# Grouped attention on one Trainium2 core: maxima and sums spread by VectorE's transposes, and a normalisation moved one step

## The chip, the cores and the metric

The kernel runs on one core of a Trainium2 chip. The metric is device time in microseconds (us) of one launch. The engines are named as the profile names them: PE is the tensor engine (PEld its weight loads), DVE the vector engine, ACT the scalar engine, POOL the GpSimd engine, SP the engine that issues most of the DMAs. PSUM is the memory that PE writes; it has 8 banks here of 512 float32 each on 128 partitions.

## The reference

Four cross-attention layers follow each other on x (4 batches, 512 queries, 256 channels), all with the same context (4 batches, 1024 rows, 512 channels). Layers 0, 2 and 3 have 16 heads of 64; four columns of their logits get a bias made from two masks. They are called masked here. Layer 1 has 16 query heads of 16 that share 4 heads of keys and values; it is called grouped.

```python
# layers 0, 2, 3
logits = einsum('bhqd,bhkd->bhqk', q, k) * scale + col_bias
probs = softmax(logits, axis=-1)
out = einsum('bhqk,bhkd->bhqd', probs, v)      # then @ Wo + bo + residual
# layer 1, after an RMS norm of x
scores = einsum('btgrd,bsgd->bgrts', qg, k) * scale
attn = softmax(scores, axis=-1)
out = einsum('bgrts,bsgd->btgrd', attn, v)     # then @ wo + residual
```

All of it is float32.

## The kernel before, in words

**Units and steps.** The work is cut into units: a pair of heads of a masked layer (8 units per layer and batch), or, in the grouped layer, one of the four query heads of each group (r) for one half of the four groups (h = 0 or 1), also 8 per batch. A written table (MASKED_TURNS, GROUPED_TURNS) sets them into 96 steps. Each step has one masked unit (g in the code); 32 of the steps have a grouped unit too (lam). The eight grouped units of a batch lie in eight steps on end, h = 0 and h = 1 in turn, so there are four such stretches. The loop at line 968 issues a step's instructions engine by engine in program order; no scheduler moves them afterwards. So the order of the calls is the order of each engine's queue.

**A step with a grouped unit.** First come the scores of the masked unit (line 643): for each of eight tiles of 128 keys PE makes the logits (L653), ACT copies them to SBUF (L663), and DVE keeps a running maximum in PSUM (L667). Then follow, woven together, the masked unit of the step before against its values (attend, L685) and the grouped unit's logits (logits_pair, L617) with their exponentials (L640). Meanwhile DVE reduces the masked maximum (L713, L721, L738), sums the exponentials of the previous unit over the partitions (reciprocal_sums, L713 to L821), scales that unit's output (L830, scale_out), spreads the maximum (L745) and subtracts it tile by tile (L750); ACT takes the exponentials (L756) and POOL adds them up (L795). Beside that PE works through a list (fill): query projections (L549), output projections (L845, added to the state by L867), the grouped unit against its values (L685, 32 columns), keys (L473), values (L515). Between these stand the four pairs of logits of the next grouped unit, which are only for its maximum (maxima_pair, L617 again, with L607 on ACT and L609 on DVE).

**The grouped maximum.** The softmax's maximum over all keys must be taken from the queries before the exponentials. max_columns (line 724) reduces the running maximum over partitions with a turning reduction (L713) and small maxima (L721, four of L730) into eight columns. In the next step, inside scores after the sixth tile (`within`, line 669), lower_queries (line 623) spreads them: sixteen small matmuls per unit against the identity (line 630) fill one PSUM bank, and DVE multiplies it by a column that is -1 in row 16 of each block of 32 and adds it to the queries (L635).

**The grouped sum.** The values have a column of ones, so row 16 of each 32 rows of the output o holds the sum of the exponentials. After an h = 1 unit both halves of o are there, and normalise_grouped runs at the end of that step (line 1160): one matmul with sel spreads row 16 over its 32 rows (sums_grouped, L705), then DVE turns it (L571), takes the reciprocal of one column in 32 (L572), turns it back (L573) and multiplies (L800). The result, ot, is projected in the next step.

**PSUM.** All eight banks belong to one tile; the class Place (line 96) hands out one or two of them, those given back longest ago first, with a preference for a bank whose neighbour is in use. back() stamps the return with a count. An instruction that writes a bank waits for the last reader of it.

Of the kernel before, what the change touches and what calls it, by code (L numbers as in the profile page):

```python
# [12 lines left out]
ALU = mybir.AluOpType  # L13
# [3 lines left out]
P = 128  # L17
B, S, C = 4, 512, 256
# [58 lines left out]
def kernel(ctx: ExitStack, tc: tile.TileContext, a: dict, out: bass.AP):  # L77
# [8 lines left out]
    def t_(shape, tag, name, bufs=1, dtype=FP):  # L86
        return sb.tile(shape, dtype, tag=tag, name=name, bufs=bufs)
# [8 lines left out]
    class Place:  # L96
# [11 lines left out]
                del free[n]  # L108
            self.ap = ps_all[:, at : at + width, :].rearrange("p n q -> p (n q)")

        def back(self):
            returns[0] += 1
            for n in self.banks:
                given_back[n] = returns[0]


    st_all = t_([P, 2, NT + 1, 2 * S], "st", "st")
# [1 line left out]
    def st_slot(n):  # L119
# [8 lines left out]
    nc.vector.memset(ones, 1.0)  # L128
    eps = t_([P, 1], "eps", "eps")
    nc.vector.memset(eps, EPS)  # L130

    sel = t_([P, 4, 32], "sel", "sel")
    nc.vector.tensor_copy(
        sel, ident.rearrange("p (g d) -> p g d", d=32)[:, :, 16:17].to_broadcast([P, 4, 32])
    )


    row16 = t_([P, 2], "row16", "row16")
    nc.vector.reduce_sum(
# [425 lines left out]
    def reciprocal_rows(out_, in_, room):  # L565


        turned = room[:, 0:S]
        short = t_([P, S // 32, 1], "short", f"short{len(turns)}")
        turns.append(0)  # L570
        nc.vector.transpose(turned, in_)  # L571
        nc.vector.reciprocal(short, turned.rearrange("p (c r) -> p c r", r=32)[:, :, 0:1])  # L572
        nc.vector.transpose(  # L573
            out_.rearrange("p (c r) -> p c r", r=32), short.to_broadcast([P, S // 32, 32])
        )
# [44 lines left out]
                )  # L620
        return ws

    def lower_queries(g):

        w = Place(1)
        m = w.ap
        for n in range(NI):
            for c in range(4):
                column = NI * (c % 2) + n
                nc.tensor.matmul(  # L630
                    m[32 * c : 32 * (c + 1), n * P : (n + 1) * P],
                    lhsT=g.mcol[:, column : column + 1].to_broadcast([P, 32]), rhs=ident,
                    start=True, stop=True,
                )
        nc.vector.scalar_tensor_tensor(g.qt, m, row16[:, 1:2], g.qt, ALU.mult, ALU.add)  # L635
        w.back()

    def exponentials_pair(g, i):
        for odd, w in enumerate(logits_pair(g, i)):
            nc.scalar.activation(g.st[2 * i + odd], w.ap, AF.Exp)  # L640
            w.back()

    def scores(g, within):
        g.st = [st_slot((NT + 1) * g.ring + t) for t in range(NT)]
        g.mx = st_slot((NT + 1) * g.ring + NT)
        g.mx_place = Place()
        for t in range(NT):

            w = Place() if t else g.mx_place
            m = w.ap  # L650
            keys = slice(t * P, (t + 1) * P)
            for j in range(2):
                nc.tensor.matmul(  # L653
                    m[:, j * S : (j + 1) * S], lhsT=g.kt[g.rows[j], keys], rhs=g.qt[g.rows[j], :],
                    start=True, stop=t > 0,
                )
            if t == 0:
                for j in range(2):
                    nc.tensor.matmul(  # L659
                        m[:, j * S : (j + 1) * S], lhsT=aug_k[g.l][g.rows[j], keys],  # L660
                        rhs=aug_q[g.rows[j], :], start=False, stop=True,
                    )
            nc.scalar.copy(g.st[t], m)  # L663
            if t:
                w.back()
                top = g.mx_place.ap
                nc.vector.tensor_tensor(top, top, g.st[t], ALU.max)  # L667
            if t == 5:
                within()

    def place_out(g, width=1):
        g.place = Place(width)
# [26 lines left out]
        nc.vector.tensor_tensor(half, half, g.po[64:128, :], ALU.add)  # L699
        g.place.back()  # L700

    def sums_grouped(g):
        g.place = Place(1)
        g.psum = g.place.ap
        nc.tensor.matmul(  # L705
            g.psum, lhsT=sel.rearrange("p g d -> p (g d)"), rhs=gq[g.b, "o"], start=True, stop=True
        )

# [12 lines left out]
        nc.vector.tensor_tensor(half, quarter[0:64, :], quarter[64:128, :], ALU.max)  # L721
        return half

    def max_columns(g):

        half = max_halves(g, g.mx)
        g.mcol = t_([P, 2 * NI], "mcol", f"mcol_{g.name}", bufs=3)
        of = half.rearrange("x (c h) -> x h c", h=4)
        for h in range(4):
            nc.vector.tensor_tensor(  # L730
                g.mcol[32 * h : 32 * (h + 1), :], of[0:32, h, :], of[32:64, h, :], ALU.max
            )

    def max_quarters(g):
        half = max_halves(g, g.mx_place.ap)
# [6 lines left out]
    def max_everywhere(g):  # L742
        g.mb_place = Place()
        g.mb = g.mb_place.ap
        nc.vector.transpose(  # L745
            g.mb.rearrange("p (b r) -> p b r", r=32), g.every.to_broadcast([P, 2 * S // 32, 32])
        )
# [55 lines left out]
    def reciprocal_sums(g):  # L803

        w = Place(1)
        quarter, half = w.ap[:, 0:32], w.ap[0:64, 32:64]
# [11 lines left out]
        w.back()  # L818
        nc.vector.reciprocal(short, short)
        g.ot = t_([P, S], "ot", f"ot_{g.name}", bufs=3)  # L820
        nc.vector.transpose(  # L821
            g.ot.rearrange("p (c r) -> p c r", r=32), short.to_broadcast([P, S // 32, 32])
        )

    def normalise(g):
        reciprocal_sums(g)
        scale_out(g)

    def scale_out(g):
# [133 lines left out]
    attended = None  # L963
    count = 0
    ready = []
    left = {b: 32 - 4 for b in range(B)}

    for n in range(len(steps) + 2):
# [46 lines left out]
        def pair(i):  # L1015
            if i == 0:
                behind_exponentials()
            maxima_pair(coming, i)
            if i == NT // 2 - 1:
                max_columns(coming)  # L1020

        if coming:
            share(coming)
# [12 lines left out]

        if g:
            g.now = NT if masked_at(g.n + 1) else 4
            scores(g, lambda: lower_queries(lam) if lam else None)

        ending = n >= len(steps) - 2
        if g1 and (g or lam):
# [1 line left out]
        if g:  # L1044
            max_quarters(g)
            if not lam:
                g.mx_place.back()
                max_everywhere(g)
        if lam:
# [103 lines left out]
        while pairs:  # L1153
            pair(pairs.pop(0)[1])
        behind_exponentials()
        if coming and not follows:
            lower_queries(coming)
# [36 lines left out]
```

## Time and profile before

| | us |
|---|---|
| median of 3 runs | 3774.69 (3774.36 to 3774.75) |
| the profiled execution | 3773.92 |
| its span in the profile | 3772.2 |
| DVE wait for L705 (L571), 4 times | 41.4 |
| 32 x L635 on DVE | 23.9 |
| 16 x L800 on DVE | 11.1 |
| 96 x L745 on DVE | 120.7 |

The profile page lists busy time by engine, a chain of work that ended last, and groups of instructions by line. A group row reads: line, engine, operation, what it writes and reads, shapes, count, then busy time and mean nanoseconds of one, then idle time of the engine just ahead of it and what ended it. A timeline row reads: start and length in us from the span's start, engine, line, operation, count, and in brackets the idle time before it and its releaser. A float32 matmul appears as two records. The granted TensorE clock is 0.998 of full speed over the whole execution.

### The profile page before, as it was taken

The page shows a single profiled execution, that of the slowest core. Times are in us where ns is not written, and L with a number is a line of the kernel's source. Part 1 is how long each engine was busy: PE and PEld are TensorE (multiplying, and loading weights), DVE is VectorE, ACT ScalarE, POOL GpSimd, SP SyncE. Part 2 cuts the span into 40 slices and gives each one's busy share as a digit, 9 for nine tenths or more (in the row PEclk, how much of TensorE's full clock was granted, in tenths as well). Part 3 has the DMA queues.
Part 4 walks back from the last instruction along what each step waited for, and adds up shares of the span by engine and source line. Part 5 has one row for each costly group of instructions (what it writes and reads, how often), then busy time and mean ns, then how long its engine had stood idle before and what let it go on. Part 6 is the DMA issues. An engine that isn't in the chain of part 4 may idle for free.

```text
span 3772.2 us, 50461 instructions
## 1 busy us (share of the span) xinstructions
PE 3723.8 (99%) x19662; PEld 1860.2 (49%) x19662; DVE 3000.4 (80%) x3928; ACT 2104.1 (56%) x2433; POOL 1625.0 (43%) x749
## 2 busy tenths in 40 slices
PE   8999999999999999999999999999999999999998
PEld 4555544445444444444555555554544445555554
DVE  6887787877887778787888888888787778888888
ACT  4555555555555555555555555555555555555554
POOL 3555333343333433333555555555333335555554
PEclk9999999999999999999999999999999999999999
DMA  2111110001000010000000110000100000000100
GB/s 68 42 31 28 39 28 21 18 20 25 22 19 21 12 33 19 22 21 18 26 26 26 43 42 24 25 26 22 26 19 23 20 24 26 26 26 26 31 25 8
DMA packets 187875, 98.71 MB, mean 26 GB/s; under 512 B 43241, under 2 KB 183529, under 8 KB 187637
## 3 DMA queue, kind: packets, MB, share of 16 engines
q1 hardware_dynamic: 182510, 82.90, 8.0%
q0 software_dynamic: 2560, 8.39, 0.8%
q10 hardware_dynamic: 2566, 4.20, 0.5%
q8 instruction: 155, 2.54, 0.3%
q14 instruction: 84, 0.68, 0.1%
HBM read 89.16 MB, written 2.10 MB: 24 GB/s over the span
## 4 chain that ended last, share of the span: by engine, by line
PE 86%; DVE 9%; issue 2%; ACT 2%; DMA 0%; DVEq 0%; POOL 0%; ACTq 0%; POOLq 0%
PE ps L515 19%; PE ps L685 18%; PE ps L473 17%; PE ps L653 12%; PE ps L617 7%; DVE ps L667 6%; PE ps L845 5%; PE ps L549 5%; ACT st L663 2%; DVE st L750 1%; PE ps L491 1%; DVE qt L635 1%; PE ps L659 1%; PE ps L705 0%; PE ps L379 0%
## 5 line engine op out<-in xcount | busy, mean ns | idle before, releaser
L795 POOL TENSOR_TENSOR st<-st 128x1024 f32<-128x1024 f32 x668 | 1580.5, 2366 | 2088.3 <-ACT st L756 2044.0
L667 DVE TENSOR_TENSOR ps<-ps,st 128x1024 f32<-128x1024 f32 x672 | 828.2, 1232 | 462.8 <-ACT st L663 405.5
L756 ACT ACTIVATE st<-st 128x1024 f32<-128x1024 f32 x768 | 783.0, 1054 | 650.0 <-DVE st L750 636.2
L750 DVE TENSOR_TENSOR st<-st,ps 128x1024 f32<-128x1024 f32 x768 | 885.9, 1214 | 3.3
L685 PE MATMUL ps<-st,v 128*64 128x512 f32 x4064 | 810.9, 598 | 0.0
L663 ACT COPY st<-ps 128x1024 f32<-128x1024 f32 x768 | 716.1, 1044 | 107.3 <-PE ps L659 82.3
L515 PEld LDWEIGHTS ps<-wv,ctx 128*128 128x128 f32 x6400 | 729.4, 192 | 80.9 <-issue 64.6
L515 PE MATMUL ps<-wv,ctx 128*128 128x128 f32 x6400 | 744.8, 276 | 0.6 <-ACT st L663 0.6
L653 PE MATMUL ps<-qt,kt 64*128 64x512 f32 x3072 | 710.5, 598 | 0.0
L473 PE MATMUL ps<-ctx,wk 128*128 128x512 f32 x1536 | 693.3, 599 | 2.2 <-ACT ctx L385 2.2
L685 PEld LDWEIGHTS ps<-st,v 128*64 128x64 f32 x4064 | 231.2, 130 | 551.5 <-issue 491.6
L473 PEld LDWEIGHTS ps<-ctx,wk 128*128 128x128 f32 x1536 | 285.7, 190 | 395.7 <-issue 375.0
L653 PEld LDWEIGHTS ps<-qt,kt 64*128 64x128 f32 x3072 | 282.7, 186 | 323.8 <-ACT st L663 142.2
L527 ACT COPY v<-ps 128x512 f32<-128x512 f32 x200 | 117.2, 586 | 538.2 <-PE ps L515 538.1
L609 DVE TENSOR_TENSOR st<-st,ps 128x1024 f32<-128x1024 f32 x224 | 273.5, 1221 | 128.1 <-ACT st L607 70.7
L640 ACT ACTIVATE st<-ps 128x1024 f32<-128x1024 f32 x256 | 248.1, 1021 | 180.2 <-PE ps L617 139.8
L617 PE MATMUL ps<-qt,kt 32*128 32x512 f32 x2048 | 302.6, 639 | 16.1 <-DVE qt L635 12.8
L845 PE MATMUL ps<-ot,wo 128*128 128x512 f32 x448 | 214.6, 607 | 0.7 <-DVE ot L830 0.7
L549 PE MATMUL ps<-x,wq 128*128 128x512 f32 x384 | 185.5, 606 | 1.1 <-ACT x L357 1.1
L617 PEld LDWEIGHTS ps<-qt,kt 32*128 32x128 f32 x2048 | 91.0, 183 | 191.0 <-ACT st L640 52.2
L478 ACT COPY kt<-ps 128x512 f32<-128x512 f32 x192 | 110.3, 574 | 102.8 <-PE ps L473 102.6
L845 PEld LDWEIGHTS ps<-ot,wo 128*128 128x128 f32 x448 | 79.8, 189 | 129.2 <-issue 120.0
(143 smaller groups left out, 1629.9 us busy)
## 6 DMA issues: line engine op xcount, KB each, us to landing
wk<-in_L_xattn_Wk_dram SPq DMA_DIRECT2D x96, 256.0 KB, 2.9
wv<-in_L_xattn_Wv_dram SPq DMA_DIRECT2D x96, 256.0 KB, 2.7
wq<-in_L_xattn_Wq_dram SPq DMA_DIRECT2D x96, 128.0 KB, 2.8
wo<-in_L_xattn_Wo_dram SPq DMA_DIRECT2D x96, 128.0 KB, 2.9
qt<-qt ACTq DMA_DIRECT2D x32, 128.0 KB, 2.2
xraw<-in_x_dram SPq DMA_DIRECT2D x3, 512.0 KB
out_dram<-out SPq DMA_DIRECT2D x3, 512.0 KB
wq<-in_L_xattn_wq_dram SPq DMA_DIRECT2D x32, 32.0 KB, 3.4
```

Of the source, the lines that this page charges most:

```text
L473: nc.tensor.matmul(m, lhsT=g.wk[:, k, :], rhs=ctx_t[g.b][:, k, n * 512 : (n + 1) * 512], start=(k == 0), stop=(k == KT - 1),)
L515: nc.tensor.matmul(m[:, t * P : (t + 1) * P], lhsT=ctx_t[g.b][:, k, (4 * n + t) * P : (4 * n + t + 1) * P], rhs=g.wv[:, k, :], start=(k == ...
L549: nc.tensor.matmul(m, lhsT=g.wq[:, k, :], rhs=x[:, k, :], start=(k == 0), stop=(k == KC - 1))
L617: nc.tensor.matmul(ws[odd].ap[:, j * S : (j + 1) * S], lhsT=g.kt[rows, i * P : (i + 1) * P], rhs=g.qt[rows, :], start=True, stop=True,)
L653: nc.tensor.matmul(m[:, j * S : (j + 1) * S], lhsT=g.kt[g.rows[j], keys], rhs=g.qt[g.rows[j], :], start=True, stop=t > 0,)
L663: nc.scalar.copy(g.st[t], m)
L667: nc.vector.tensor_tensor(top, top, g.st[t], ALU.max)
L685: nc.tensor.matmul(g.po[at, :], lhsT=g.v[:, t, rows], rhs=g.st[t][:, j * S : (j + 1) * S], start=(t == first), stop=(t == last),)
L750: nc.vector.tensor_tensor(g.st[t], g.st[t], g.mb, ALU.subtract)
L756: nc.scalar.activation(st, st, AF.Exp)
L795: nc.gpsimd.tensor_tensor(g.acc, g.st[0] if t == 1 else g.acc, g.st[t], ALU.add)
L845: nc.tensor.matmul(m[:, k * S : (k + 1) * S], lhsT=g.wo[:, k * P : (k + 1) * P], rhs=g.ot, start=True, stop=True,)
```

## The change

Three things change in the code. The maximum's spreading is done by DVE at once, in the step that computed it: the four small maxima write a tile `every` of 16 columns instead of the eight columns, a transpose writes it, each column repeated 32 times, into a PSUM bank, and the update of the queries follows. So the call inside scores goes. The bank is taken after the small maxima, and given back with a count that is two later. The grouped sum's spreading loses its matmul with sel: DVE turns o itself into a bank, takes the reciprocal of row 16's column, turns it back into the bank, and multiplies. And that normalisation is no longer at the end of the h = 1 step: the unit is put on a list (turned), and the next step does it right behind reciprocal_sums in the same PSUM bank (or, in a step without a grouped unit, in a bank of its own).

```diff
-        def back(self):
+        def back(self, late=0):
             returns[0] += 1
             for n in self.banks:
-                given_back[n] = returns[0]
+                given_back[n] = returns[0] + late
...
-    def lower_queries(g):
-
-        w = Place(1)
-        m = w.ap
-        for n in range(NI):
-            for c in range(4):
-                column = NI * (c % 2) + n
-                nc.tensor.matmul(
-                    m[32 * c : 32 * (c + 1), n * P : (n + 1) * P],
-                    lhsT=g.mcol[:, column : column + 1].to_broadcast([P, 32]), rhs=ident,
-                    start=True, stop=True,
-                )
-        nc.vector.scalar_tensor_tensor(g.qt, m, row16[:, 1:2], g.qt, ALU.mult, ALU.add)
-        w.back()
...
-            if t == 5:
-                within()
...
-    def max_columns(g):
+    def lower_queries(g):
+
 
         half = max_halves(g, g.mx)
-        g.mcol = t_([P, 2 * NI], "mcol", f"mcol_{g.name}", bufs=3)
-        of = half.rearrange("x (c h) -> x h c", h=4)
-        for h in range(4):
+        every = t_([P, S // 32, 1], "every1", f"every1_{g.name}")
+        for c in range(4):
+            cols = slice(c % 2 * S // 32, (c % 2 + 1) * S // 32)
             nc.vector.tensor_tensor(
-                g.mcol[32 * h : 32 * (h + 1), :], of[0:32, h, :], of[32:64, h, :], ALU.max
+                every[32 * c : 32 * (c + 1), :, 0], half[0:32, cols], half[32:64, cols], ALU.max
             )
+        w = Place(1)
+        m = w.ap
+        nc.vector.transpose(
+            m.rearrange("p (b r) -> p b r", r=32), every.to_broadcast([P, S // 32, 32])
+        )
+        nc.vector.scalar_tensor_tensor(g.qt, m, row16[:, 1:2], g.qt, ALU.mult, ALU.add)
+        w.back(late=2)
...
-    def normalise_grouped(g, room):
+    def normalise_grouped(g, m):
+
+        o = gq[g.b, "o"]
+        short = t_([P, S // 32, 1], "short", f"short_{g.name}")
+        nc.vector.transpose(m, o)
+        nc.vector.reciprocal(short, m.rearrange("p (c r) -> p c r", r=32)[:, :, 16:17])
+        nc.vector.transpose(
+            m.rearrange("p (c r) -> p c r", r=32), short.to_broadcast([P, S // 32, 32])
+        )
         g.ot = t_([P, S], "ot", f"ot_{g.name}", bufs=3)
-        reciprocal_rows(g.ot, g.psum, room)
-        nc.vector.tensor_tensor(g.ot, gq[g.b, "o"], g.ot, ALU.mult)
-        g.place.back()
+        nc.vector.tensor_tensor(g.ot, o, m, ALU.mult)
...
+        if turned or lam and g1:
+
+            w = Place(1)
+            if lam and g1:
+                reciprocal_sums(g1, w.ap)
+            for each in turned:
+                normalise_grouped(each, w.ap)
+            w.back()
+        turned.clear()
         if lam:
-            if g1:
-                reciprocal_sums(g1)
...
         if lam and lam.h == 1:
-            sums_grouped(lam)
-            normalise_grouped(lam, st_slot((NT + 1) * (count % 2) + NT))
+            turned.append(lam)
             ready.append(lam)
```

The function sums_grouped, the tile sel and the copy that fills it at the start are removed.

More of the change, by code (lines that the diff above doesn't have):

```diff
@@ L130 @@
     nc.vector.memset(eps, EPS)
-    sel = t_([P, 4, 32], "sel", "sel")
-    nc.vector.tensor_copy(
-        sel, ident.rearrange("p (g d) -> p g d", d=32)[:, :, 16:17].to_broadcast([P, 4, 32])
-    )
     row16 = t_([P, 2], "row16", "row16")
@@ L621, in logits_pair @@
         return ws
-    def lower_queries(g):
-        w = Place(1)
-        m = w.ap
-        for n in range(NI):
-            for c in range(4):
-                column = NI * (c % 2) + n
-                nc.tensor.matmul(
-                    m[32 * c : 32 * (c + 1), n * P : (n + 1) * P],
-                    lhsT=g.mcol[:, column : column + 1].to_broadcast([P, 32]), rhs=ident,
-                    start=True, stop=True,
-                )
-        nc.vector.scalar_tensor_tensor(g.qt, m, row16[:, 1:2], g.qt, ALU.mult, ALU.add)
-        w.back()
     def exponentials_pair(g, i):
@@ L641, in exponentials_pair, with scores @@
             w.back()
-    def scores(g, within):
+    def scores(g):
         g.st = [st_slot((NT + 1) * g.ring + t) for t in range(NT)]
@@ L700, in keep_odd @@
         g.place.back()
[L702 to L707, printed above, removed]
     def over_quarter(out_, of, op):
@@ L795, in running_sum, with reciprocal_sums @@
         nc.gpsimd.tensor_tensor(g.acc, g.st[0] if t == 1 else g.acc, g.st[t], ALU.add)
-    def normalise_grouped(g, room):
-        g.ot = t_([P, S], "ot", f"ot_{g.name}", bufs=3)
-        reciprocal_rows(g.ot, g.psum, room)
-        nc.vector.tensor_tensor(g.ot, gq[g.b, "o"], g.ot, ALU.mult)
-        g.place.back()
-    def reciprocal_sums(g):
-        w = Place(1)
-        quarter, half = w.ap[:, 0:32], w.ap[0:64, 32:64]
+    def normalise_grouped(g, m):
[6 more added lines that the diff above has]
+        )
+        g.ot = t_([P, S], "ot", f"ot_{g.name}", bufs=3)
+        nc.vector.tensor_tensor(g.ot, o, m, ALU.mult)
+    def reciprocal_sums(g, m):
+        quarter, half = m[:, 0:32], m[0:64, 32:64]
         other = t_([64, 32], "other", f"other_{g.name}")
@@ L817, in reciprocal_sums @@
             )
-        w.back()
         nc.vector.reciprocal(short, short)
@@ L825, in normalise @@
     def normalise(g):
-        reciprocal_sums(g)
+        w = Place(1)
+        reciprocal_sums(g, w.ap)
+        w.back()
         scale_out(g)
@@ L965 @@
     ready = []
+    turned = []
     left = {b: 32 - 4 for b in range(B)}
@@ L1019, in pair @@
             if i == NT // 2 - 1:
-                max_columns(coming)
+                lower_queries(coming)
         if coming:
@@ L1038 @@
             g.now = NT if masked_at(g.n + 1) else 4
-            scores(g, lambda: lower_queries(lam) if lam else None)
+            scores(g)
         ending = n >= len(steps) - 2
@@ L1048 @@
                 max_everywhere(g)
+        if turned or lam and g1:
+            w = Place(1)
+            if lam and g1:
+                reciprocal_sums(g1, w.ap)
+            for each in turned:
+                normalise_grouped(each, w.ap)
+            w.back()
+        turned.clear()
         if lam:
-            if g1:
-                reciprocal_sums(g1)
             for i in range(NT // 2):
@@ L1155 @@
         behind_exponentials()
-        if coming and not follows:
-            lower_queries(coming)
         if lam and lam.h == 1:
-            sums_grouped(lam)
-            normalise_grouped(lam, st_slot((NT + 1) * (count % 2) + NT))
+            turned.append(lam)
             ready.append(lam)
```

## The prediction

> **What bounds the kernel now.** I read the busy shares first, then the chain that ended last, then PE's waits, then the timeline of single steps. The busy shares and the chain:
>
> ```profile
> PE 3723.8 (99%) x19662; PEld 1860.2 (49%) x19662; DVE 3000.4 (80%) x3928; ACT 2104.1 (56%) x2433; POOL 1625.0 (43%) x749
> ...
> PE 86%; DVE 9%; issue 2%; ACT 2%; DMA 0%; DVEq 0%; POOL 0%; ACTq 0%; POOLq 0%
> ```
>
> PE sets the end nearly everywhere. DVE holds 9% of the chain, mostly L667. The waits of PE and the groups of the two removed products say where the change touches PE:
>
> ```profile
> PE ps L617 <- DVE qt L635: 12.8, 32, 0.7
> ...
> L630 PE MATMUL ps<-ident,mcol 128*32 128x128 f32 x1024 | 34.6, 276 | 0.0
> ...
> L705 PE MATMUL ps<-o,sel 128*128 128x512 f32 x32 | 16.4, 594 | 0.0
> ```
>
> Each of the 32 grouped steps has one wait for L635, and it is PE's longest by total. Now one step (it starts with its first score matmul, L653, at 472.27), its PE, DVE and ACT rows (start, length, what):
>
> ```profile
> 477.83 1.08 PE L630 MATMUL ps<-ident,mcol 128*32 128x128 f32 x32
> 480.76 1.94 PE L685 MATMUL ps<-st,v 128*64 128x512 f32 x8
> 483.12 1.14 PE L617 MATMUL ps<-qt,kt 32*128 32x512 f32 x8 [0.42 <-DVE qt L635]
> 493.27 1.98 PE L549 MATMUL ps<-x,wq 128*128 128x512 f32 x4
> 520.49 1.02 PE L705 MATMUL ps<-o,sel 128*128 128x512 f32 x2
> 521.44 1.13 PE L653 MATMUL ps<-qt,kt 64*128 64x512 f32 x4
> ...
> 482.22 0.75 DVE L635 SCALAR_TENSOR_TENSOR qt<-ps,row,qt 128x512 f32<-128x512 f32 x1
> 482.89 2.56 DVE L667 TENSOR_TENSOR ps<-ps,st 128x1024 f32<-128x1024 f32 x2
> 492.32 0.69 DVE L830 TENSOR_TENSOR ot<-ps,ot 128x512 f32<-128x512 f32 x1 [0.89 <-PE ps L685]
> ...
> 473.65 5.59 ACT L663 COPY st<-ps 128x1024 f32<-128x1024 f32 x6 [0.69 <-PE ps L659]
> ```
>
> The reader is to see the queue on DVE: L635 stands behind five running maxima (L667), so the grouped logits (L617) start late, and everything on PE up to L549 follows at fixed distances.
>
> **What a removed product is worth.** The busy column gives 34.6 + 16.4 = 51.0 us. The Trainium skill (Perfetto Trace Analysis, "Identifying the Most-Contended Engine") says that busy time of pipelined matmuls is no good measure. The starts agree: L705 to the next L653 is 521.44 - 520.49 = 0.95, where the row says 1.02; L630 to the next start was 1.01. By starts it is 32 x 1.01 + 16 x 0.95 = 47.5 us. I take starts.
>
> **1. Products and the update leave the scores (32 steps).** With no L630 the last two score tiles wait only for copies 4 and 5 of ACT. The copies run from 473.65 at 5.59 / 6 = 0.93 each: copy 5 ends 478.3, copy 6 479.2, copy 8 481.1. A matmul follows the copy that frees its bank by about 0.43 (an estimate from tile six: copy 3 ends at 476.45, its matmuls start at about 476.9). So the last tile starts at 478.7, and L685, which in the changed program takes half of copy 6's place, at 479.7 instead of 480.76. Eight of L685 take 1.87, so L617 comes at 481.55, which copy 8 also allows (481.1 + 0.43). Before: 483.12. **Gain 1.57**, of which 1.01 is the product and 0.56 idle. What is late next is the copies, then ACT's exponentials; the later blocks (1.87 and 1.07 apart) keep the gain. DVE gains 0.67 (482.22 to 482.89), and the 0.89 wait of L830 goes, as L685 ends earlier: its subtractions come 1.55 earlier, so DVE and ACT keep up with PE to the end of the step.
>
> Here the skill speaks against it: the same page ("Optimization Strategy") says a gap that repeats can mean too little PSUM. Then the 12.8 us would stay. The row names DVE qt as releaser 32 times, and the data wait really goes; I side with the row. But part 3 is such a bank wait, newly made.
>
> **2. Turning at the step's end (32 times).** Four small maxima replace four of L730 (182 or 165 against 163 ns: nothing). A turn into PSUM of 128x512 is added: 711 (L573) to 716 ns (L571), or half of L745's 1257; plus L635's 0.75 moved here: 1.5 us of DVE. It issues no DMA. What hides it: DVE idles 3.9 to 7.5 us before the next step's first L667. After an h = 1 step it idles only 0.5, but there 2.48 us (L571 to L800, 521.83 to 524.31) leave. Queued behind the turn are the next maxima; PE's third to fifth score tile waits for its bank, and by my times has 0 to 0.4 us too little once in a pair of steps, where DVE sets the pace anyway. Cost 0; with no cover, up to 1.5 each. The bank given back with late=2 is to keep the value product from waiting for it.
>
> **3. Normalising moves one step (16 times).** L705 goes from the end of every h = 1 step: gain 0.95. Its four DVE instructions (0.72 + 0.25 + 0.71 + 0.69 with gaps = 2.48) now stand behind the masked sums' turn (L821) and ahead of L830. The weight loads on SP and the clears on POOL that lie between the old and the new place touch none of its tiles; no DMA of its own moves. In the changed program the next query product (L549) goes to this very bank and waits for the last of the four. The step from 521.44 (DVE, PE and ACT rows):
>
> ```profile
> 539.76 0.71 DVE L821 STREAM_TRANSPOSE ot<-short 128x512 f32<-128x512 f32 x1
> 543.25 3.48 DVE L750 TENSOR_TENSOR st<-st,ps 128x1024 f32<-128x1024 f32 x3
> ...
> 542.31 1.98 PE L549 MATMUL ps<-x,wq 128*128 128x512 f32 x4
> 557.84 1.14 PE L617 MATMUL ps<-qt,kt 32*128 32x512 f32 x8
> ...
> 556.66 0.99 ACT L607 COPY st<-ps 128x1024 f32<-128x1024 f32 x1
> ```
>
> Measured from this step's start: L821 ends at 540.47 - 0.66 (L635 gone) = 539.81; plus 2.51 is 542.32; plus 0.43 for PE is 542.75 against 542.31. So the gain of part 1 is eaten whole, and 0.44 more. Behind it L830, L745 and the subtractions come 1.0 later, ACT's exponentials and L607 too (558.7), and the second half of L617's second pair, which needs L607's bank, comes at 559.1 against 558.3. **Loss about 0.8** in the twelve steps that follow an h = 1 step and have a grouped unit (bounds -0.5, if PE makes the bank wait up elsewhere, and 2.5).
>
> In the four steps after a batch's last grouped unit no lower_queries was there to remove, and the four instructions stand behind L745:
>
> ```profile
> 828.69 1.26 DVE L745 STREAM_TRANSPOSE ps<-every 128x1024 f32<-128x1024 f32 x1
> 827.86 3.70 PE L845 MATMUL ps<-ot,wo 128*128 128x512 f32 x8
> ```
>
> The second half of L845 multiplies just this ot. It started near 829.7; now 829.95 + 2.48 + 0.43 = 832.9. **Loss 3.2** each (bounds 2.4 and 4).
>
> **4. Start.** The copy of sel (0.31) leaves DVE's chain at the start: 0.3.
>
> **Sum.** 4 first steps x 1.57 = 6.3; 16 h = 1 steps x 2.52 = 40.3; 0.3; together 46.9 gained. Lost: 12 x 0.8 + 4 x 3.2 = 22.4. Net 24.5 us. The profiled execution took 3773.92 (span 3772.2): 3749.4. The median is 0.8 higher, which I leave inside the range. **Forecast 3749 us**, 0.7% under the median; 0.2%, 7.5 us, is about what this measurement can tell from no change.
>
> **Rivals.** A: the hand-over costs nothing, because PE recovers behind the waits; all 46.9 arrive: 3727. For it: PE has small gaps to lose in each step. Against: the wait stands in the program, and PE is full behind it. 22%. B: the gain of part 1 comes by half only (another bank wait replaces L635): 32 x 0.6 + 15.2 - 22.4 = 12: 3762, 12%; with nearly nothing left of it, 3774: 6%. C, the other side: the hand-over grows. Place: L549 behind the four instructions, then the late subtractions, ACT's exponentials, the banks of the grouped maxima, and the turn at the end so late that the next scores wait. It decides from 46.9 / 16 = 2.9 us per hand-over (mine is 1.4 on the mean) and is slower by 0.2% from 3.4. At 4.2: 3773.9 - 46.9 + 67 = 3794. Against: DVE idles 4 to 7 us at the end of just these steps. 5%. The forecast itself: 55%, its own range 3740 to 3759.
>
> **Chances and range.** Faster 0.22 + 0.55 + 0.11 = 0.88; no change 0.07; slower 0.05. 3724 to 3763 takes in the forecast, A, and most of B's first half.
>
> **What would show it.** In the changed profile: L630, L705 and the wait L617 <- qt gone; L617 about 9.2 us after a step's first L653 (10.9 before); h = 1 steps 2.5 us shorter; in twelve steps the query product waits 2 us or so for the multiply of normalise_grouped, and those steps keep their length; in four steps the projection waits 3 us for it. Wrong, if those twelve shorten as well (A), or if their end waits for the turn too (C).

## The result, and the profile after

The changed kernel takes 3749.63 us (median of 4 runs, 3744.01 to 3751.03); beside it the kernel before took 3774.53 (4 runs, 3774.03 to 3774.75). The ratio is 0.9931, 95% interval 0.9914 to 0.9949. The profiled execution took 3749.48, its span is 3747.7 against 3772.2.

Most lines have new numbers: the scores' matmul L653 is now L632, their copy L663 is L642, the running maximum L667 is L646, the grouped logits L617 are L611, the query product L549 is L543, the projection L845 is L829 and its addition L867 is L851, attend's L685 is L662, the maximum's turn L745 is L723, the subtraction L750 is L728, keep_odd's L699 is L676, the keys' product L473 is L467, the maxima L609 of the grouped unit are L603, the turn of the masked sums L821 is L803 and the scaling L830 is L814. New are L706 and L709 (turn and update of the queries) and L779 to L785 (normalise_grouped).

First the busy shares of the changed kernel, and the shares of its chain that ended last:

```profile
PE 3683.2 (98%) x18606; PEld 1836.7 (49%) x18606; DVE 3025.1 (81%) x3959; ACT 2109.2 (56%) x2433; POOL 1625.9 (43%) x749
...
PE 89%; DVE 8%; ACT 1%; issue 1%; DMA 0%; POOL 0%; DVEq 0%; ACTq 0%; POOLq 0%
```

PE has 1056 matmul records fewer and 40.6 us less busy time, but the span is only 24.5 us shorter. DVE still holds 8% of the chain. The waits of PE in the changed kernel (total us, times, longest) name where the rest went:

```profile
PE ps L543 <- DVE ot L785: 15.5, 10, 1.6
PE ps L829 <- issue: 10.3, 4, 2.6
...
PE ps L543 <- issue: 3.3, 2, 1.7
```

The wait of the grouped logits for the update, 12.8 us before, is gone. In its place the query product waits for the last of the four normalising instructions, L785; in two of the twelve steps the releaser is not named ("issue"). And four times the projection waits 2.6 us.

A total hides that gains and losses lie in different steps. So I took the start of each step's first score matmul (L653 before, L632 after) from both profiles. Its distance to the next start is the step's length, and the table gives the change of that length against before:

| step | number | change of one, mean us | all, us |
|---|---|---|---|
| first grouped step of a batch | 4 | -1.69 | -6.8 |
| h = 1, more units follow | 12 | -2.55 | -30.7 |
| last h = 1 step of a batch | 4 | -2.67 | -10.7 |
| h = 0 step behind an h = 1 step | 12 | +0.53 | +6.3 |
| step after a batch's last grouped unit | 4 | +4.09 | +16.4 |
| the other steps | 59 | 0.00 | +0.2 |

The sum is -25.2; the last step and the end together are 0.7 us longer.

Now one of the twelve h = 0 steps, the one that the prediction followed. It starts at 517.31; the rows are PE's, with one of its weight loads (PEld), then DVE's:

```profile
517.31 1.13 PE L632 MATMUL ps<-qt,kt 64*128 64x512 f32 x4
535.60 1.14 PE L611 MATMUL ps<-qt,kt 32*128 32x512 f32 x8
538.32 1.98 PE L543 MATMUL ps<-x,wq 128*128 128x512 f32 x4 [1.58 <-DVE ot L785]
550.86 1.78 PE L611 MATMUL ps<-qt,kt 32*128 32x512 f32 x8
551.52 0.30 PEld L611 LDWEIGHTS ps<-qt,kt 32*128 32x128 f32 x4 [0.36 <-DVE st L728]
...
520.65 9.26 DVE L646 TENSOR_TENSOR ps<-ps,st 128x1024 f32<-128x1024 f32 x7 [0.56 <-ACT st L642]
535.16 0.71 DVE L803 STREAM_TRANSPOSE ot<-short 128x512 f32<-128x512 f32 x1
535.80 0.68 DVE L779 STREAM_TRANSPOSE ps<-o 128x512 f32<-128x512 f32 x1
537.57 0.69 DVE L785 TENSOR_TENSOR ot<-o,ps 128x512 f32<-128x512 f32 x1
538.18 0.68 DVE L814 TENSOR_TENSOR ot<-ps,ot 128x512 f32<-128x512 f32 x1
540.06 3.48 DVE L728 TENSOR_TENSOR st<-st,ps 128x1024 f32<-128x1024 f32 x3
546.86 4.61 DVE L728 TENSOR_TENSOR st<-st,ps 128x1024 f32<-128x1024 f32 x4
551.71 0.69 DVE L676 TENSOR_TENSOR o<-o,ps 64x512 f32<-64x512 f32 x1 [0.24 <-ACT o L672]
```

Two things are to be seen. L543 starts 1.58 us late, right behind L785. And between the start of the running maxima (520.65) and the end of the last subtraction (551.47) no row of DVE has an idle time in front, those left out here neither: 30.8 us without a gap. L611 at 550.86 takes 1.78 us instead of 1.14: the weights of its second half come at 551.52, just behind the end of the last subtraction (L728, 551.47), which gives back the bank that this half needs, and the two halves do not run side by side. Which of the two holds the step, the bank of L543 or DVE's row, the prediction did not separate; the experiments do.

Last the step after a batch's last grouped unit (the second batch), PE's rows:

```profile
1289.75 1.98 PE L829 MATMUL ps<-ot,wo 128*128 128x512 f32 x4
1294.31 2.50 PE L829 MATMUL ps<-ot,wo 128*128 128x512 f32 x4 [2.58 <-issue]
1296.60 3.08 PE L543 MATMUL ps<-x,wq 128*128 128x512 f32 x4
```

The second half of L829 multiplies the late ot and waits 2.58 us. But then PE is also slow: these four matmuls take 2.29 us to the next start and the next four 2.91, where the same two rows take 1.79 and 1.72 after the first batch. The view of the same stretches (us, busy times, then the granted TensorE clock, third from the end) says why:

```profile
1294.31:1296.60 2.29, 2.29 (x5) 0.98 (x6) 2.29 (x3) 1.06 (x1) 0.00 (x0) 0.78 0.00 0
1296.60:1299.51 2.91, 2.91 (x5) 1.20 (x4) 2.91 (x3) 1.06 (x1) 0.74 (x1) 0.59 0.00 0
```

The clock lost there is 0.22 x 2.29 + 0.41 x 2.91 = 1.7 us. With the stretches laid closer it is one piece of 3.41 us at half the clock, which begins 1.28 us after the wait's end:

```profile
1292.17:1295.58 3.41, 1.27 (x3) 0.68 (x4) 3.31 (x6) 0.21 (x1) 0.00 (x0) 1.00 0.00 0
1295.59:1298.99 3.40, 3.40 (x5) 1.35 (x4) 3.40 (x4) 1.90 (x2) 0.22 (x1) 0.50 0.00 0
```

The four steps are 2.82, 4.51, 4.51 and 4.51 us longer: 2.82 for the wait, and in three of them 1.69 more for the clock.

### The profile page after: what moved, and what is told of

Same layout as the page of the kernel before. It is cut to its first block, busy times and chain, and to the rows that moved or that the text cites. A ratio compares the mean times of both kernels' runs of the same rounds, so it can differ in the third digit from the quotient of the medians.

```text
span 3747.7 us, 48412 instructions
## 1 busy us (share of the span) xinstructions
PE 3683.2 (98%) x18606; PEld 1836.7 (49%) x18606; DVE 3025.1 (81%) x3959; ACT 2109.2 (56%) x2433; POOL 1625.9 (43%) x749
## 4 chain that ended last, share of the span: by engine, by line
PE 89%; DVE 8%; ACT 1%; issue 1%; DMA 0%; POOL 0%; DVEq 0%; ACTq 0%; POOLq 0%
PE ps L509 19%; PE ps L662 18%; PE ps L467 17%; PE ps L632 15%; PE ps L611 6%; PE ps L829 5%; PE ps L543 5%; DVE ps L646 4%; DVE st L728 1%; ACT st L642 1%; PE ps L485 1%; PE ps L638 1%; DVE quarter L683 1%; DVE ps L683 0%; PE ps L373 0%
## 5 line engine op out<-in xcount | busy, mean ns | idle before, releaser
L646 DVE TENSOR_TENSOR ps<-ps,st 128x1024 f32<-128x1024 f32 x672 | 828.6, 1233 | 483.4 <-ACT st L642 422.1
L728 DVE TENSOR_TENSOR st<-st,ps 128x1024 f32<-128x1024 f32 x768 | 886.3, 1216 | 3.2
L662 PE MATMUL ps<-st,v 128*64 128x512 f32 x4064 | 810.9, 598 | 0.0
L509 PEld LDWEIGHTS ps<-wv,ctx 128*128 128x128 f32 x6400 | 729.4, 192 | 80.9 <-issue 63.8
L642 ACT COPY st<-ps 128x1024 f32<-128x1024 f32 x768 | 713.1, 1049 | 68.6 <-PE ps L638 67.5
L509 PE MATMUL ps<-wv,ctx 128*128 128x128 f32 x6400 | 744.8, 276 | 0.6 <-ACT st L642 0.6
L632 PE MATMUL ps<-qt,kt 64*128 64x512 f32 x3072 | 702.5, 596 | 0.3 <-ACT st L642 0.3
L467 PE MATMUL ps<-ctx,wk 128*128 128x512 f32 x1536 | 694.9, 600 | 2.2 <-ACT ctx L379 2.2
L662 PEld LDWEIGHTS ps<-st,v 128*64 128x64 f32 x4064 | 231.2, 130 | 551.5 <-issue 460.5
L467 PEld LDWEIGHTS ps<-ctx,wk 128*128 128x128 f32 x1536 | 286.6, 191 | 398.0 <-issue 375.0
L632 PEld LDWEIGHTS ps<-qt,kt 64*128 64x128 f32 x3072 | 284.5, 186 | 324.4 <-ACT st L642 155.6
L603 DVE TENSOR_TENSOR st<-st,ps 128x1024 f32<-128x1024 f32 x224 | 273.6, 1221 | 118.7 <-ACT st L601 65.9
L611 PE MATMUL ps<-qt,kt 32*128 32x512 f32 x2048 | 308.0, 639 | 3.2 <-DVE ot L814 3.2
L829 PE MATMUL ps<-ot,wo 128*128 128x512 f32 x448 | 218.2, 614 | 11.1 <-issue 10.3
L543 PE MATMUL ps<-x,wq 128*128 128x512 f32 x384 | 186.8, 609 | 16.6 <-DVE ot L785 15.5
L611 PEld LDWEIGHTS ps<-qt,kt 32*128 32x128 f32 x2048 | 93.2, 183 | 179.1 <-ACT st L619 51.9
L829 PEld LDWEIGHTS ps<-ot,wo 128*128 128x128 f32 x448 | 79.8, 190 | 141.2 <-issue 134.8
```

Source lines behind the costliest of these rows:

```text
L467: nc.tensor.matmul(m, lhsT=g.wk[:, k, :], rhs=ctx_t[g.b][:, k, n * 512 : (n + 1) * 512], start=(k == 0), stop=(k == KT - 1),)
L509: nc.tensor.matmul(m[:, t * P : (t + 1) * P], lhsT=ctx_t[g.b][:, k, (4 * n + t) * P : (4 * n + t + 1) * P], rhs=g.wv[:, k, :], start=(k == ...
L543: nc.tensor.matmul(m, lhsT=g.wq[:, k, :], rhs=x[:, k, :], start=(k == 0), stop=(k == KC - 1))
L611: nc.tensor.matmul(ws[odd].ap[:, j * S : (j + 1) * S], lhsT=g.kt[rows, i * P : (i + 1) * P], rhs=g.qt[rows, :], start=True, stop=True,)
L632: nc.tensor.matmul(m[:, j * S : (j + 1) * S], lhsT=g.kt[g.rows[j], keys], rhs=g.qt[g.rows[j], :], start=True, stop=t > 0,)
L662: nc.tensor.matmul(g.po[at, :], lhsT=g.v[:, t, rows], rhs=g.st[t][:, j * S : (j + 1) * S], start=(t == first), stop=(t == last),)
```

## The experiments

The changes of a step's length against before, mean us per step, worked out from each kernel's profile as above (the 59 other steps stay within 0.4 us everywhere):

| kernel | time, us | first (4) | h = 1 (12) | last h = 1 (4) | h = 0 behind h = 1 (12) | after the last (4) |
|---|---|---|---|---|---|---|
| the change | 3749.6 | -1.69 | -2.55 | -2.67 | +0.53 | +4.09 |
| spread_only | 3731.2 | -1.69 | -1.69 | -1.81 | -0.75 | 0.00 |
| norm_only | 3791.4 | 0.00 | -0.86 | -0.86 | +1.16 | +4.07 |
| norm_in_ot | 3753.7 | -1.70 | -2.56 | -2.67 | +0.90 | +3.78 |
| norm_at_end | 3726.9 | -1.69 | -2.55 | -2.67 | +0.04 | 0.00 |
| norm_in_hole | 3709.9 | -1.70 | -2.55 | -2.67 | -1.41 | 0.00 |
| extra_turn | 3757.9 | -1.70 | -2.55 | -2.67 | +1.29 | +3.66 |
| late0 | 3752.3 | -1.69 | -2.55 | -2.67 | +0.92 | +3.66 |
| queries_first | 3744.1 | -1.70 | -2.56 | -2.67 | +0.53 | +2.44 |
| outs_later | 3742.4 | -1.70 | -2.55 | -2.67 | +0.53 | +2.26 |

The last column and the times of kernels that have a loss there swing by 1.7 us per step with the pieces of half clock just seen, here called clock windows; so do two of the twelve steps of norm_in_ot. The other columns repeat to 0.02 us where the code is the same.

### The two halves of the change, each alone: spread_only and norm_only

In spread_only the grouped sums keep their product with sel and their place:

```diff
...
-        if turned or lam and g1:
+        if lam and g1:
             w = Place(1)
-            if lam and g1:
-                reciprocal_sums(g1, w.ap)
-            for each in turned:
-                normalise_grouped(each, w.ap)
+            reciprocal_sums(g1, w.ap)
             w.back()
...
-            turned.append(lam)
+            sums_grouped(lam)
+            normalise_grouped(lam, st_slot((NT + 1) * (count % 2) + NT))
```

> The spreading of the maximum by VectorE's turn at the step's end alone; the grouped sums are spread by the product with sel and normalised at the end of the h = 1 step, as before. Theory (the move of the normalising cost all that is missing): every one of the 32 grouped steps loses 1.6 to 1.7 us, no query product waits for a normalising, the steps after a batch's last grouped unit keep their length: 32 x 1.65 = 53 us less than before's 3774.5, 3722 us. Rival (the turn and the update at the end have no cover: before them only 0.5 us of DVE were idle after an h = 1 step): the twelve steps behind an h = 1 step lose 1.0 to 1.5 us of that again, 3734 to 3740 us.

Measured: 3731.24 us, ratio 0.9884 (0.9868 to 0.9899). The first and h = 1 steps gain the 1.7 of the theory, but the twelve behind them only 0.75: the rival has its loss, 0.94 each in the mean, and the total lies between the two sums. The turn and the update at the step's end do have a price, when the old normalising still stands behind them. In spread_only's timeline (the scores are L638 there, the running maximum L652, the old normalising ends with L791):

```profile
518.77 1.13 PE L638 MATMUL ps<-qt,kt 64*128 64x512 f32 x4
...
522.39 0.69 DVE L791 TENSOR_TENSOR ot<-o,ot 128x512 f32<-128x512 f32 x1
523.00 3.90 DVE L652 TENSOR_TENSOR ps<-ps,st 128x1024 f32<-128x1024 f32 x3
```

The first running maximum starts 4.23 us after the step's start; in the changed kernel it is 520.65 - 517.31 = 3.34. The difference, 0.89, is near the mean loss of 0.94; the single steps vary around it, with gains from 0.0 to 1.1.

In norm_only the maximum is spread by the old matmuls inside the scores, and the normalising is that of the change.

> The normalising alone: VectorE turns the grouped sums, one step later, in the bank of the masked sums; the maximum is spread by the sixteen matmuls inside the scores, as before. Theory: h = 1 steps 0.95 us shorter, the twelve steps behind them about 2.2 us longer (query product behind the multiply of normalise_grouped), the four behind a batch's last unit about 4.1 longer: -15 + 26 + 16 = +27, 3802 us. Rival (the hand-over costs PE next to nothing and the gain of the spreading was small): the twelve steps 0 to 0.5 us longer, 3775 to 3782 us.

Measured: 3791.38 us, ratio 1.0044 (1.003 to 1.0057), slower than before. The steps after the last unit lose what the theory says, the h = 1 steps gain 0.86, the twelve lose 1.16, half of my 2.2, and so the total lies between the two sums. The two halves nearly add up: -0.75 + 1.16 = 0.41 against 0.53 in the twelve steps; in time -43.4 + 16.8 = -26.6 against -24.9. So **the moved normalising took away 17 to 18 us of what the spreading brings**.

### Bank or queue: norm_in_ot

The same four instructions at the same place of DVE's queue, but without a PSUM bank:

```diff
-        nc.vector.transpose(m, o)
-        nc.vector.reciprocal(short, m.rearrange("p (c r) -> p c r", r=32)[:, :, 16:17])
+        g.ot = t_([P, S], "ot", f"ot_{g.name}", bufs=3)
+        nc.vector.transpose(g.ot, o)
+        nc.vector.reciprocal(short, g.ot.rearrange("p (c r) -> p c r", r=32)[:, :, 16:17])
         nc.vector.transpose(
-            m.rearrange("p (c r) -> p c r", r=32), short.to_broadcast([P, S // 32, 32])
+            g.ot.rearrange("p (c r) -> p c r", r=32), short.to_broadcast([P, S // 32, 32])
         )
-        g.ot = t_([P, S], "ot", f"ot_{g.name}", bufs=3)
-        nc.vector.tensor_tensor(g.ot, o, m, ALU.mult)
+        nc.vector.tensor_tensor(g.ot, o, g.ot, ALU.mult)
...
```

> The changed kernel with the same four normalising instructions at the same place of DVE's queue, but they work in ot itself instead of the PSUM bank of the masked sums. So the query product waits for the masked sums alone, while all that is queued on DVE behind the four stays as late as it was. Theory (the bank's wait is what the twelve steps pay): they lose the 1.6 us wait and become about 0.5 to 1 us shorter than before instead of 0.5 longer; in all 3730 to 3737 us. Rival (the late subtractions and exponentials are what they pay): PE waits as long, only later in the step, 3747 to 3750 us. The four steps behind a batch's last unit stay 4 us longer in both, since there the projection waits for the data.

Measured: 3753.70 us, ratio 0.9943 (0.993 to 0.9957): no gain over the change, and my theory falls. PE's rows of the same step, and below them PE's waits in this kernel:

```profile
516.83 1.13 PE L632 MATMUL ps<-qt,kt 64*128 64x512 f32 x4
536.19 1.98 PE L543 MATMUL ps<-x,wq 128*128 128x512 f32 x4
548.74 1.13 PE L611 MATMUL ps<-qt,kt 32*128 32x512 f32 x4
551.01 1.13 PE L611 MATMUL ps<-qt,kt 32*128 32x512 f32 x4 [1.15 <-DVE st L728]
```

```profile
PE ps L467 <- DVE st L728: 7.0, 6, 1.2
...
PE ps L611 <- DVE st L728: 6.5, 6, 1.2
```

L543 no longer waits: it starts 19.36 us into the step instead of 21.01. Yet the second half of L611 starts no earlier, because its bank is that of the maximum (g.mb), and the last subtraction, L728, gives it back. In all twelve steps PE now waits for the last subtraction, six times at L611 and six times at the keys' product L467: 1.15 to 1.18 us in eleven of them, 0.63 in one. **The bank wait was only the first place where DVE's lateness showed.** Two of the twelve steps (+2.40 and +4.04) are long by clock windows behind this very wait; the other ten are 0.44 us longer, in the changed kernel the same ten 0.47.

### Longer by one turn: extra_turn

If DVE's row paces the step, each instruction put into it must cost its own time. One more turn of the maximum's first half, which writes the same values again, in the twelve steps:

```diff
+        again = turned[0] if lam and turned else None
...
             if g:
                 max_everywhere(g)
+                if again:
+                    nc.vector.transpose(
+                        g.mb.rearrange("p (b r) -> p b r", r=32)[:, 0 : S // 32],
+                        g.every[:, 0 : S // 32, :].to_broadcast([P, S // 32, 32]),
+                    )
```

> The changed kernel with one more turn of 128x512 on DVE (0.7 us), ahead of the subtractions of the twelve steps behind an h = 1 step; no wait of PE is tied to it beside the one on the subtractions. Theory (DVE's unbroken row from the first running maximum to the last subtraction paces these steps): each of them is 0.7 us longer, 8.4 us in all, 3758 us. Rival (the bank wait of the query product paces them and DVE has slack behind it): 0 to 0.2 us each, 3749 to 3752 us.

Measured: 3757.87 us, ratio 0.9957 (0.9941 to 0.9972). The twelve steps went from +0.53 to +1.29: 0.76 each for an instruction of 0.7. No slack is left: this is the queue's own price.

### Other places in DVE's queue: norm_at_end and norm_in_hole

Both use the instructions of norm_in_ot. norm_at_end issues them at the end of the h = 1 step, behind the update of the queries:

```diff
...
-            turned.append(lam)
+            normalise_grouped(lam)
```

> The changed kernel, but the four normalising instructions (VectorE's turn of the sums, in ot) stand at the end of the h = 1 step, behind the update of the queries, instead of a step later. Theory (the lateness alone cost what was lost): all 32 grouped steps 1.6 us shorter, the 16 h = 1 steps another 0.95, the four steps behind them keep their length: 52 + 15 = 67 us under before, 3707 us. Rival (DVE has no room for 4 us there: 0.5 idle plus 2.5 of the old normalising before the next running maximum): the twelve next steps lose 1.0 to 1.5 us again and the four after a batch some too, 3720 to 3727 us.

Measured: 3726.94 us, ratio 0.9873 (0.9858 to 0.9888). The four steps after the last unit lose nothing. The twelve come to +0.04, 1.73 short of the gain of the first steps, more than the rival's 1.0 to 1.5, while the four that it wanted slower too are not. The total is the rival's. In its timeline:

```profile
517.98 1.13 PE L632 MATMUL ps<-qt,kt 64*128 64x512 f32 x4
...
522.45 0.69 DVE L785 TENSOR_TENSOR ot<-o,ot 128x512 f32<-128x512 f32 x1
523.06 9.25 DVE L646 TENSOR_TENSOR ps<-ps,st 128x1024 f32<-128x1024 f32 x7
```

The running maximum starts 5.08 us into the step, 1.74 later than the 3.34 of the changed kernel, and the loss of the twelve is 1.73 in the mean. That these steps start 0.86 earlier (no L705) doesn't help: the end of DVE's queue stays where it was.

norm_in_hole puts them where DVE is idle. In an h = 1 step DVE ends o with keep_odd, and then has 2.5 us with nothing to do until ACT has copied the first logits of the next unit's maximum (2.52 in norm_at_end's timeline):

```diff
...
             late.append(lambda: keep_odd(lam))
+            if lam.h == 1:
+                late.append(lambda: normalise_grouped(lam))
...
-            turned.append(lam)
```

> The changed kernel with the four normalising instructions (in ot) right behind the addition that completes o, inside the h = 1 step, where DVE then idles 2.5 us until the next unit's first maximum. Theory (in the twelve steps behind an h = 1 step DVE works without a gap from the first running maximum to the last subtraction and paces PE, so what counts is which place of DVE's queue pays): grouped steps keep all that the removed products gave, -1.7 in the four first, -2.55 in the twelve h = 1 steps, -1.7 in the twelve behind them, -2.67 in the four last, 0 in the steps after them: 68 us under before's 3774.5, 3706 us. Rival (the idle 2.5 us are needed, the maxima of the next unit come late and PE's banks with them): the twelve h = 1 steps shorten by 1.0 to 1.5 us only, 3718 to 3725 us.

Measured: **3709.86 us**, ratio 0.983 (0.9817 to 0.9844), the fastest of all, faster than both kernels; the theory's sum was 3706. DVE's rows, ahead of them the end of the additions, and the start of the next step:

```profile
502.30 0.69 DVE L676 TENSOR_TENSOR o<-o,ps 64x512 f32<-64x512 f32 x1
503.02 0.71 DVE L780 STREAM_TRANSPOSE ot<-o 128x512 f32<-128x512 f32 x1
...
504.80 1.00 DVE L785 TENSOR_TENSOR ot<-o,ot 128x512 f32<-128x512 f32 x1
505.84 1.22 DVE L603 TENSOR_TENSOR st<-st,ps 128x1024 f32<-128x1024 f32 x1
...
518.04 1.13 PE L632 MATMUL ps<-qt,kt 64*128 64x512 f32 x4
521.38 2.57 DVE L646 TENSOR_TENSOR ps<-ps,st 128x1024 f32<-128x1024 f32 x2 [0.56 <-ACT st L642]
```

The four fit in: they take 2.78 us here, so L603 comes 0.3 us later, and DVE's next idle takes that up (0.41 us, in norm_at_end 0.75). The running maximum is back at 3.34 us. The twelve h = 1 steps keep their 2.55, the twelve behind them gain 1.41 and not quite 1.7. What takes the last 0.3 was not tried; DVE's row has no idle time from the first running maximum to the last subtraction in eleven of the twelve here either.

All runs together say the same. Counted from the step's start and averaged over the twelve steps, the last subtraction ends at 32.0 us in norm_in_hole, 32.9 in spread_only, 33.72 in norm_at_end, 34.20 in the changed kernel, 34.58 in late0 (below), 34.79 in norm_only and 34.97 in extra_turn. The lengths stand in the same order: -1.41, -0.75, +0.04, +0.53, +0.92, +1.16 and +1.29. From norm_at_end to extra_turn both grow by 1.25.

In the chain of this kernel DVE's share is 4%:

```profile
PE 94%; DVE 4%; ACT 1%; issue 1%; DMA 0%; POOL 0%; DVEq 0%; ACTq 0%; POOLq 0%
```

### The bank taken late: late0

```diff
-        w.back(late=2)
+        w.back()
```

> The changed kernel with the bank of the maximum's turn given back with the plain count, so that the third score tile of the next step takes it instead of the fourth. Theory (that tile waits for the update of the queries, which ends about 2.8 us after the step's start in the steps behind an h = 1 step, but DVE paces those steps anyway): PE waits 0.5 to 1 us there and makes it up, 3749 to 3753 us. Rival (the late bank was worth its name): 0.8 us for each of twelve steps and something in the others, 3757 to 3765 us.

Measured: 3752.30 us, ratio 0.9941 (0.9927 to 0.9954); the interval overlaps that of the change. In the profile the twelve steps are 0.39 us longer than in the changed kernel. The score tile that takes the bank waits for the update, as the theory has it, shown by PE's rows and, below, by the sum of its waits:

```profile
519.98 4.56 PE L632 MATMUL ps<-qt,kt 64*128 64x512 f32 x20 [0.64 <-DVE qt L709]
```

```profile
PE ps L632 <- DVE qt L709: 7.8, 12, 0.7
```

PE makes up only part of the 0.65: 12 x 0.39, about 5 us of the change's gain, come from the late count. The medians are only 2.7 us apart: the profile of late0 has a clock window less in the steps of the next section (1.7 us).

### The four steps after the last unit: queries_first and outs_later

In these steps PE's list was changed, first the query products ahead of the projections:

```diff
+        had_turned = bool(turned)
...
+        elif had_turned:
+            fill[0:0] = of_queries
         else:
             fill += of_queries
```

> The changed kernel, but in the four steps after a batch's last grouped unit PE's list starts with the query products and comes to the output projections after them. Theory (these steps lose 4.1 us because the projection needs the ot that DVE multiplies late): the wait is covered by 1.9 to 3.7 us of query products, the four steps lose 0.5 to 1.5 us instead of 4.1, in all 11 to 14 us under the changed kernel's 3749.6: 3736 to 3739 us. Rival (DVE's lateness paces PE there as in the steps with a grouped unit): the wait comes back later in the step, 3746 to 3750 us.

Measured: 3744.09 us, ratio 0.9919 (0.9904 to 0.9935), 5.5 under the change and not the 11 to 14 expected. The reason is in the list: only two of the four steps have such a query product, and one each. In these two:

```profile
817.17 1.98 PE L543 MATMUL ps<-x,wq 128*128 128x512 f32 x4
819.00 1.88 PE L829 MATMUL ps<-ot,wo 128*128 128x512 f32 x4
821.84 1.95 PE L829 MATMUL ps<-ot,wo 128*128 128x512 f32 x4 [0.97 <-issue]
```

The wait shrinks from 2.58 to 0.97 and the step from 2.82, without a clock window, to 1.20 us over before: it does not come back later. So here the data is late, not DVE's whole queue. The move itself is worth 2 x 1.6 us; in this profile two of the four steps are also without the clock window that they had in the changed kernel's, so part of the 5.5 us is clock. The other run moves the projections behind the keys' products:

```diff
+        had_turned = bool(turned)
...
+        waiting = len(fill)
...
+        if had_turned and not lam:
+            fill = fill[waiting:] + fill[:waiting]
```

> The changed kernel, but in the four steps after a batch's last grouped unit PE takes the keys' products (7 us) ahead of the output projections. Theory (these steps wait only for the late ot: 2.8 us of idle, and in some of them 1.7 us more from a window of 3.4 us at half the TensorE clock that the idle sets off): no wait, no such window, the four steps come back to their length in the kernel before, 11 to 18 us under the changed kernel on the same chip: 3733 to 3737 us. Rival (DVE's late subtractions pace these steps as they pace the steps with a grouped unit): the four steps stay 2 to 2.5 us longer than before, 3743 to 3746 us.

Measured: 3742.39 us, ratio 0.9915 (0.9897 to 0.9933). The total lies in neither range. In the first two of the four steps the loss is 0.00, as the theory says. In the others it is 1.55 and 7.49, by waits of the edit's own making, which neither theory had: both are for the addition to the state (L851), which now comes late on DVE. In the third step a value product (L509) waits 1.14 us for it. In the fourth the next layer's first query product, which reads the state, follows the projection at once, and two clock windows (6.8 us) come with its wait:

```profile
3082.07 3.78 PE L543 MATMUL ps<-x,wq 128*128 128x512 f32 x4 [5.12 <-DVE x L851]
```

The order of these projections is held from both sides, by ot ahead of them and by the state behind them.

### The changed kernel once more: after_again

> The changed kernel once more, on the same chip as the run beside it. Theory (the half-clock windows fall by chance on the idle of the four steps): the steps after a batch's last unit are 2.8 us longer than before, or 2.8 + 1.7 where a window falls, and all other steps as in its first profile; 3744 to 3751 us. Rival (the 1.7 us are fixed in the program): the same three of the four steps have it.

Measured: 3751.34 us, ratio 0.9938 (0.992 to 0.9955). The twelve steps and all others repeat to 0.02 us but one, which is 0.17 longer. The four last ones are 2.82, 4.51, 4.51 and 4.52 us longer: the same three steps have the clock window as in the first profile, as the rival has it.

The granted clock on record says what decides it here. Within each profile that has several clock windows, they begin a whole number of times 3.413 us apart, to 0.01 us: in the first profile at 1295.59, 1770.04 and 3080.76, which is 139 and 384 times 3.413. So there is a fixed grid, and each long idle can be laid on it. Seven profiles, after_again's among them, have waits of 2.6 to 2.9 us in these steps, 26 in all. Sixteen have at least 2.04 us within one piece of the grid, and the next piece is at half clock each time; the other ten are cut by a border of the grid so that no piece has more than 1.90, and none is followed by it. The wait of the first batch (819.33 to 821.91) is cut at 821.13, into 1.80 and 0.78. The grid lay at nearly the same place of both profiles of the changed kernel (0.23 us apart from the span's start), hence the same three steps; in the other kernels it lies elsewhere. What sets its place in a run is not shown. The run of 3744.0 has no trace; an execution without the three windows would take about 3749.5 - 3 x 1.7 = 3744.4, an estimate from these figures.

## Why the prediction came out as it did

**Worth of the removed products: right, a little low.** The wait of L617 is gone; L611 starts 479.84 - 470.69 = 9.15 us into the h = 1 step, where the prediction had 9.2. The gain of the first steps is 1.69 against 1.57. The bank shortage that could have kept the wait did not appear: no other wait took its place in those steps. L705 was worth 2.55 - 1.69 = 0.86, not 0.95.

**The turn at the end costs nothing: right only with part 3.** In the changed kernel the 2.48 us of the old normalising make room, and the running maximum starts at 3.34 us as before. Where they stay (spread_only) the turn costs 0.9. It is no free work, it took the place of other work, and the prediction said on which condition.

**The hand-over: size near, its visible wait misleading.** Predicted +0.8 for each of the twelve steps, measured 0.81 in five of them, 0.27 to 0.53 in seven, 0.53 in the mean. The chain of the prediction had both a bank wait at L549 and, behind late subtractions and ACT, a late second pair of L617 that needs the bank of L607. The late subtractions were right. The bank is another: that of the masked maximum, which the last subtraction gives back itself, one call of L617 earlier in this step, in the half that starts at 551.52. norm_in_ot and extra_turn show that DVE's row carries the loss alone: by starts of the step, the last subtraction ended at 33.20 before (L750, 550.04 + 4.60 - 521.44) and ends at 34.16 after (551.47 - 517.31). Four instructions came (538.18 - 535.80 = 2.38), L635 and the wait of L830 went (0.66 and 0.89), and the rest of the row takes 0.13 longer; 0.96 are left, and PE had a little slack for them. What would have corrected the prediction's account: the row of DVE in the trace of before, which from L667 to L750 has one gap, just that 0.89.

**The four steps after the last unit: the mechanism right, the size off.** Predicted 3.2 each; the wait costs 2.82, but in three of them 1.69 come on top through the clock, for which the prediction has no term: 4.09 in the mean. The wait itself was put too high by the 0.43 us between a release and the matmul behind it. That figure came from copies of ACT at a place where PE shows no wait; behind L785 it is 0.06 us at L543 (538.26 to 538.32) and 0.10 at L829 (1294.21 to 1294.31).

**The total: near by luck.** The term of these four steps was too small by 3.6 us in all, the one of the twelve steps too large by 3.3; they cancel. That the sum, 24.5, is the measured one to 0.1 us says nothing of the terms, and the changed kernel's own medians, 3749.6 and 3751.3, differ by more.

**The start:** the 0.3 us of the sel copy cannot be told apart; the first score matmul starts 33.9 us after the span's start against 33.8, and between 33.3 and 34.9 in the other kernels.

**The rivals.** A (PE recovers behind the waits) failed, since PE wasn't what paced those steps. B (half the gain) has no support in the first steps. Its sum was also off: it gives 0.6 us to all 32 steps, where the forecast's sum counts part 1 in 20 only, and half of 1.57 is 0.79. With 20 x 0.79 it comes to about 3765, above the range. C (the hand-over grows to 2.9 us) did not come: it cost (6.3 + 16.4) / 16 = 1.4 us, just the mean of the prediction. Of its places the late subtractions and a bank behind them were right; the next scores did not wait for the turn. norm_only shows that without the spreading the hand-over alone makes the kernel slower than before.

## What to carry to other kernels

Before an instruction is moved, look at the whole row of its engine between two fixed points: a row without a gap, whose end another engine waits for, charges most or all of the time of what is put in, wherever the wait then shows, and a row with a gap of the right length took it for nothing here. Here four instructions of 2.4 us cost about 40 us more (3749.6 against 3709.9) in one place of the queue than in another, with the bound engine's work unchanged. And a wait removed by a new buffer proves nothing until the next use of the same engine's results starts earlier too.

## What the runs showed of the hardware

A short idle of PE can be followed by a lower TensorE clock. After an idle of 2.58 us the granted clock was 0.50 for 3.41 us, and 1.7 us were lost. It does not follow always: after the first batch the same 2.58 us were followed by a clock of 1.00. For the idles of 2.6 to 2.9 us their place on the grid of 3.413 us decided it in all 26 cases: at least 2.04 us in one piece of the grid, or at most 1.90.

For shorter idles the runs give no such line. Eleven idles in norm_in_ot take 1.15 to 1.18 us, ten of them whole within one piece of the grid; two of the ten were followed by half clock, one by a single piece of it and one by two. The rows are of one of the two, the first with the idle ahead of it in brackets, the second with the granted clock third from the end:

```profile
1596.56 1.13 PE L611 MATMUL ps<-qt,kt 32*128 32x512 f32 x4 [1.18 <-DVE st L728]
1597.62:1600.69 3.07, 3.07 (x7) 0.82 (x5) 1.15 (x1) 1.89 (x3) 2.99 (x2) 0.61 0.00 0
```

What sets these two apart stays open.

The Trainium skill (TensorE: Matmul & The Clock Gate, "HAM oscillation — how this bites in real kernels") sets the danger at idle gaps of more than about 3.4 us. By that rule none of these waits would have cost more than itself; the trace shows up to 1.7 us more for idles of 2.58, and 1.6 and 3.2 us more in the two steps with an idle of 1.18, so a short wait on the engine that is otherwise full can cost more than its length.
